# Copying two columns per VectorE instruction with and/xor and register-addressed scalars, in a graph-network kernel on one core

## The chip, the core and the metric

The kernel runs on one core of a Trainium2 chip. The metric is the device time of one execution in microseconds (us); lower is better. An engine is named as in the profile: PE (TensorE), PEld (its weight loads), DVE (VectorE), ACT (ScalarE), POOL (GpSimd) and SP (SyncE). A name with a q behind it (DVEq) is the sequencer of that engine, which carries out register loads, register operations and semaphore waits itself and hands the rest to the engine.

## What is computed

One layer of message passing over a graph with 12500 nodes of 64 features and 400000 edges with 16 attributes, followed by a residual sum and a layer norm. The edges are sorted by their target `dst`.

```python
m_in = concatenate([x[src], x[dst], edge_attr], axis=-1)
h = silu(m_in @ W1 + b1)
messages = silu(h @ W2 + b2)
agg = segment_sum(messages, dst, num_segments=12500)
y = silu(concatenate([x, agg], axis=-1) @ W3 + b3)
return layernorm(x + y)
```

What matters here is `x[src]`: the sources are random, so 400000 rows (or columns of the transposed x) have to be fetched by index.

## The kernel before

The edges are cut into 3125 tiles of 128, and eight tiles make an octet; the main loop runs over 391 octets (`NO`) and works ahead and behind: octet o is gathered three octets earlier, its first layer runs in iteration o, the second layer in o + 1, the sum over targets (`add_up`) in o + 2, and `add_window` adds that to the node sums `agg` in o + 4. The order of PE, ScalarE, VectorE and SyncE is written out by hand (`manual_schedule`): on each engine, instructions run in the order in which the loop calls them. What waits for what is kept by semaphores that the framework sets for every read after a write, also between two instructions of one engine.

The rows of x[src] come in three ways.

- `gather` (L373): POOL starts an indirect DMA for each tile, which fetches 128 rows from a table in DRAM. From octet 12 (`RAW`) that is `pa`, which already holds x times the first part of W1; the rows are added to the first layer's PSUM tile by products with the identity (L454).
- `columns`: for one pair of tiles (256 edges) in about every second octet there is no gather. All of x, transposed, is resident in SBUF twice (`xs`: partitions 0 to 63 and again 64 to 127, one column of 64 values per node). For each edge, ScalarE or VectorE copies that node's column into a tile `cx`, from an address in a register. PE multiplies `cx` by `w1d` (L451). `pairs` lists the octets that take a pair; `RATE` is the number of columns copied per octet, by both engines together, and so sets how often a pair is ready.
- `rows`: SyncE fetches single rows for a further 23 pairs by DMAs of 256 bytes (L324), 16 an octet.

`columns(o, eng, part)` is called twice per octet and engine: VectorE's part 0 comes after `compare_dst` (tile `oh`, L424), its part 1 after `window_copy` (`xw`, L402) and `compare_nodes` (`eh`, L430); ScalarE's part 0 comes ahead of the first layer's Silu (`h`, L458), part 1 ahead of the second layer's (`m`, L473). `ACOLS` and `VCOLS` give the columns of each part. A part is cut into pieces of at most 16 columns, for the first, and 8 for the others (`LOADS`), and where the tile of 128 edges ends. Per piece there is one register load (TENSOR_LOAD at L290) that reads the addresses from `cxi` into registers, and then one instruction per column: on VectorE a `tensor_reduce` (max over an axis of one element) of 4 bytes as uint8 (L297), on ScalarE a `copy` (L299).

`address` (L359) makes byte addresses of the indices on VectorE two octets earlier. `bases` (L381) loads the registers of four windows, every fourth octet. The nodes' own last layer and norm run in groups within the loop (L514 to L547): `node_stats` takes `bn_stats` (L533) and `bn_aggr` (L534) in turn, `divide` (L547) is a `tensor_scalar` with two scalars of one value per partition. `wrow` is a PSUM tile that holds small rows for the comparisons (`wn`, `row`); the gathers rotate through five buffers.

Of the kernel before, what the change touches and what calls it, by code (L numbers as in the profile page):

```python
# [11 lines left out]
I32 = mybir.dt.int32  # L12
U8 = mybir.dt.uint8
AF = mybir.ActivationFunctionType
OP = mybir.AluOpType
AX = mybir.AxisListType
PSUM = bass.MemoryType.PSUM
DRAM = bass.MemoryType.DRAM
ENG = mybir.EngineType

P = 128
# [3 lines left out]
S = 48  # L25
# [2 lines left out]
AHEAD = 3  # L28
RAW = 12
TABLES = 7  # L30
ACOLS = (32, 28)
VCOLS = (32, 32)
ROWS = 16
LOADS = (16, 8)
XBASE = (0, 64 << 18)
XADDR = 36864
LAG = CT * P // 32
# [7 lines left out]
def kernel(  # L45
# [43 lines left out]
    with ExitStack() as inner:  # L89
        windows(inner, tc, ident, badi, pa, x, xt, src_c, src_row, dst_c, dst_row, attr_t, dst_2, attr_2, base, w1, b1, w2, b2, w3, b3, out, edges)  # L90
# [7 lines left out]
def windows(ctx, tc, ident, badi, pa, x, xt, src_c, src_row, dst_c, dst_row, attr_t, dst_2, attr_2, base, w1, b1, w2, b2, w3, b3, out, edges):  # L98
    nc = tc.nc
    N, D = x.shape  # L100
# [3 lines left out]
    NO = base.shape[1]  # L104
# [31 lines left out]
    for s in range(2):  # L136
        h = slice(s * D, (s + 1) * D)
# [10 lines left out]
    for s in range(2):  # L148
        h = slice(s * D, (s + 1) * D)
# [6 lines left out]
    for s in range(3):  # L156
        part = const.tile([1, D], BF16, name=f"part{s}")
# [55 lines left out]
    wrow = wps.tile([P, 512], F32, name="wrow")  # L213
    wn, row = wrow[:, :NO], wrow[:, NO:NO + S]
    nc.vector.tensor_copy(row, rowi)
    pb = mis.tile([P, NO], F32, name="mm")
    nc.tensor.matmul(pb, ones, bf, start=True, stop=True)
    nc.vector.tensor_copy(wb, pb)
# [17 lines left out]
    for k in range(3):  # L236
        t = fast.tile([P, P], F32, name=f"xw{k}")
# [10 lines left out]
    with tc.tile_pool(name="gat", bufs=AHEAD + 2) as gat, tc.tile_pool(name="drp", bufs=2) as drp, \  # L248
# [11 lines left out]

        RATE = sum(ACOLS) + sum(VCOLS)
        pairs = []
        while True:
            o = RAW + -(-2 * P * (len(pairs) + 1) // RATE) + 1
# [3 lines left out]
        cols, indices = {}, {}  # L268
        xb = xs.bitcast(U8)

        def columns(o, eng, part):
            if o < RAW:
                return
            lo = (o - RAW) * RATE
            if eng == ENG.Activation:
                lo, n = lo + sum(ACOLS[:part]), ACOLS[part]
            else:
                lo, n = lo + sum(ACOLS) + sum(VCOLS[:part]), VCOLS[part]
            hi, todo = lo + n, n
            while lo < hi:  # L280
                j, e0 = lo // (2 * P), lo % (2 * P)
                if j >= len(pairs):
                    return
                n = min(hi - lo, P - e0 % P, LOADS[lo > hi - todo])
                if pairs[j] not in cols:
                    cols[pairs[j]] = cx.tile([P, P], F32, name="cx")
                t = cols[pairs[j]].bitcast(U8)
                s = e0 // P
                h = slice(s * D, (s + 1) * D)
                _, regs = nc.values_load_multi_w_load_instructions(  # L290
                    indices[j][0:1, e0:e0 + n], engines=(eng,), min_val=XBASE[s] + XADDR,
                    max_val=XBASE[s] + XADDR + 4 * (N - 1), skip_runtime_bounds_check_because="src names a node")
                for e, r in zip(range(e0 % P, e0 % P + n), regs):
                    to, frm = t[h, 4 * e:4 * e + 4], xb[h, ds(r - (XBASE[s] + XADDR), 4)]
                    if eng == ENG.DVE:

                        nc.vector.tensor_reduce(to, frm[:, :, None], AX.X, OP.max)  # L297
                    else:
                        nc.scalar.copy(to, frm)  # L299
                lo += n  # L300


        rpairs = []
        while True:
            o = RAW + -(-2 * P * (len(rpairs) + 1) // ROWS) + 1
# [128 lines left out]
        def first_layer(o):  # L434
            c, t0, n, first, last = octs[o]
            n2 = n + n % 2
            k = n2 // 2
            ga = got.pop(o)
            oh, eh = hots.pop(o)
            p1 = ps1.tile([P, OT // 2, P], F32, name="p1")  # L440
            nc.tensor.matmul(p1[:, :k], xw[o % 3], oh, start=True, stop=False, skip_group_check=True)  # L441
            if o < RAW:
                pt = mis.tile([P, OT // 2, P], F32, name="mm")
                for i in range(k):
                    nc.tensor.matmul(pt[:, i, :], ga[:, 2 * i:2 * i + 2, :].rearrange("p s d -> p (s d)"), ident,  # L445
                                     start=True, stop=True)
                xg = work.tile([P, OT // 2, P], F32, name="m")
                nc.vector.tensor_copy(xg[:, :k], pt[:, :k])
                nc.tensor.matmul(p1[:, :k], w1d, xg[:, :k], start=False, stop=True, skip_group_check=True)
            if o in pairs:  # L450
                nc.tensor.matmul(p1[:, 0, :], w1d, cols.pop(o), start=False, stop=False, skip_group_check=True)  # L451
            for i in range(1 if o in pairs else 0, k if o >= RAW else 0):
                g2 = single.pop(o) if o in rpairs and i == 1 else ga[:, 2 * i:2 * i + 2, :]
                nc.tensor.matmul(p1[:, i, :], g2.rearrange("p s d -> p (s d)"), ident,  # L454
                                 start=False, stop=(i == k - 1), skip_group_check=True)
            columns(o, ENG.Activation, 0)
            h = work.tile([P, OT // 2, P], F32, name="h")
            nc.scalar.activation(h[:, :k], p1[:, :k], AF.Silu, bias=b1s)  # L458
            made[o] = h, eh

        def second_layer(o):
            c, t0, n, first, last = octs[o]
            n2 = n + n % 2
            k = n2 // 2
            h, eh = made.pop(o)
            p2 = ps2.tile([P, OT, D], F32, name="p2")
            nc.tensor.matmul(p2[:, :n2, :], one3, b2r[:, :n2, :], start=True, stop=False, skip_group_check=True)  # L467
            for i in range(k):
                nc.tensor.matmul(p2[:, 2 * i:2 * i + 2, :].rearrange("p s d -> p (s d)"), h[:, i, :], w2d,  # L469
                                 start=False, stop=(i == k - 1), skip_group_check=True)  # L470
            columns(o + 1, ENG.Activation, 1)
            m = work.tile([P, OT, D], F32, name="m")
            nc.scalar.activation(m[:, :n2], p2[:, :n2], AF.Silu)  # L473
            made[o] = m, eh
# [85 lines left out]
        todo = {}  # L560
# [7 lines left out]
        for q in range(early):  # L568
            o = lead[due[q]] + 3 if q < rest else NO
# [4 lines left out]
        for q0, q1 in batches:  # L574
            o = lead[due[q1 - 1]] + 3
# [22 lines left out]
        with tc.manual_schedule(engines={ENG.PE, ENG.Activation, ENG.DVE, ENG.SP}):  # L598
            compare_dst(0)
            compare_nodes(0)  # L600
            for o in range(NO + 1):
# [3 lines left out]
                for k in parts[3 * o - 3:3 * o] if o else []:  # L605
                    n = min(XC, NP - k)
# [33 lines left out]
                if o + 1 < NO:  # L640
                    compare_dst(o + 1)
                columns(o, ENG.DVE, 0)
                if o < NO:
                    first_layer(o)
# [10 lines left out]
                if 30 <= o < 30 + 2 * LP and o % 2 == 0:  # L655
                    k = (o - 30) // 2
                    part = rel[:, k * TILES // LP:(k + 1) * TILES // LP]
# [307 lines left out]
```

## Time and profile before

| | |
|---|---|
| median of 3 runs | 3438.62 us (3430.88 to 3440.32) |
| the profiled execution's own time | 5200.1 us |
| its span, first to last instruction | 5197.9 us |
| busy in the span: PE, PEld | 2932.5 us, 2075.4 us |
| busy in the span: VectorE | 2641.3 us, 26395 instructions |
| busy in the span: ScalarE | 2906.1 us, 23402 instructions |
| busy in the span: POOL | 2565.3 us, 2724 instructions |
| gathers by POOL (from `pa` and from x) | 2619 and 96, mean 0.94 us each |
| column copies, VectorE and ScalarE | 24032 and 22560 |
| granted TensorE clock, mean | 0.629 |

The profiled execution took much longer than the others; a busy share of its span is not the share of a normal execution. In a row of the groups, the name says which tile is written and from what (`cx<-xs`), then come the count, the busy time, the mean duration of one, and the idle time of that engine just ahead of these instructions with what ended it. A duration runs from the start of an instruction[...], and the next one can start before that; what one costs in a row of equal ones is the time from start to start, the pitch. "issue" is idle time for which the profile shows no releaser.

### The profile page before, as it was taken

Reading aid. Unit: us, or ns where it says so; the run is one execution under the profiler, and the core shown is the slowest. Engines: PE = TensorE matmul, PEld = TensorE weight load, DVE = VectorE, ACT = ScalarE, POOL = GpSimd, SP = SyncE. Lnnn points to the kernel's source line nnn. Section 1 sums busy time; section 2 is a strip of 40 time slices with the busy share of each in tenths; the row PEclk is TensorE's granted clock in tenths of the full one; section 3 lists DMA queues with packets and bytes.
Section 4 is the critical chain, followed back from the end, with each engine's and each line's share of the span. In section 5 each row is a group of like instructions: output and inputs, shape, how many; then the busy total and the mean of one; then the engine's idle time right before and its main releaser. Section 6 shows DMA issues by size and latency. Waiting matters only on the chain. (4 is left out here: it accounts for less than half of the span.)

```text
span 5197.9 us, 107486 instructions
## 1 busy us (share of the span) xinstructions
PE 2932.5 (56%) x15131; PEld 2075.4 (40%) x15131; DVE 2641.3 (51%) x26395; ACT 2906.1 (56%) x23402; POOL 2565.3 (49%) x2724
## 2 busy tenths in 40 slices
PE   5655655555555555555564655656555555555566
PEld 3443434434433344343343434434433343344344
DVE  1255555545555555555555555555555555555555
ACT  1255555555555655655556565555556555655555
POOL 5544454454444544445444444545454444555453
PEclk7666565666666666666656566565656666665656
DMA  4321111211211121122112211211211221121121
GB/s 85 86 46 39 40 39 40 47 39 40 46 42 43 40 46 40 40 43 42 41 40 49 43 40 42 44 39 40 47 40 40 44 47 40 40 47 39 40 46 40
DMA packets 203943, 229.98 MB, mean 44 GB/s; under 512 B 133612, under 2 KB 141988, under 8 KB 202324
## 3 DMA queue, kind: packets, MB, share of 16 engines
q1 hardware_dynamic: 101528, 122.61, 10.5%
q0 software_dynamic: 86880, 89.14, 9.1%
q10 hardware_dynamic: 14812, 11.26, 0.9%
q14 instruction: 595, 4.87, 0.3%
q8 instruction: 128, 2.10, 0.2%
HBM read 216.36 MB, written 6.40 MB: 43 GB/s over the span
## 5 line engine op out<-in xcount | busy, mean ns | idle before, releaser
L373 POOL DMA_INDIRECT ga<-pa,sc x2619 | 2472.2, 944 | 2516.1 <-PE p L454 1699.8
L299 ACT COPY cx<-xs 64x4 uint8 x22560 | 2404.2, 188 | 1406.1 <-issue 1362.4
L297 DVE TENSOR_REDUCE cx<-xs 64x4 uint8 x24032 | 1910.3, 150 | 1806.6 <-issue 1740.9
L441 PE MATMUL p<-oh,xw 128*128 128x512 f32 (+1 forms) x782 | 772.4, 1089 | 1529.3 <-DVE xw L402 727.6
L441 PEld LDWEIGHTS p<-oh,xw 128*128 128x128 f32 x782 | 187.1, 297 | 1637.1 <-DVE xw L402 776.3
L482 PE MATMUL pg<-eh,m 128*64 128x48 f32 x6250 | 363.0, 277 | 588.6 <-ACT m L473 174.1
L454 PEld LDWEIGHTS p<-ident,ga 128*128 128x128 f32 x2620 | 591.3, 314 | 194.9 <-issue 193.6
L469 PE MATMUL p<-w2d,h 128*128 128x128 f32 x3126 | 642.0, 369 | 1.5 <-issue 1.4
L469 PEld LDWEIGHTS p<-w2d,h 128*128 128x128 f32 x3126 | 545.3, 263 | 133.0 <-issue 133.0
L454 PE MATMUL p<-ident,ga 128*128 128x128 f32 x2620 | 593.2, 397 | 0.0
L482 PEld LDWEIGHTS pg<-eh,m 128*64 128x64 f32 x6250 | 312.1, 189 | 680.2 <-issue 342.2
L473 ACT ACTIVATE m<-p 128x512 f32<-128x512 f32 x391 | 231.8, 593 | 474.9 <-remote 308.9
L458 ACT ACTIVATE h<-p,b1s 128x512 f32<-128x512 f32 x391 | 267.4, 684 | 319.0 <-remote 138.6
L402 DVE TENSOR_TENSOR xw<-mm,mask 96x128 f32<-96x128 f32 x391 | 110.4, 282 | 439.9 <-issue 392.4
L397 PE MATMUL mm<-w1bb,xr 64*96 64x128 f32 x782 | 241.0, 401 | 72.6 <-ACT z L523 49.9
L424 DVE TENSOR_TENSOR oh<-dr,wrow 96x512 f32<-96x512 int32 x391 | 263.6, 674 | 6.3 <-issue 3.5
L430 DVE TENSOR_TENSOR eh<-wrow,dc 128x384 f32<-128x384 f32 x391 | 213.2, 545 | 42.2 <-issue 42.2
L467 PE MATMUL p<-b2r,one 3*128 3x512 bf16 x391 | 194.5, 498 | 0.0
L451 PEld LDWEIGHTS p<-cx,w1d 128*128 128x128 f32 x364 | 116.0, 319 | 175.4 <-issue 175.4
L397 PEld LDWEIGHTS mm<-w1bb,xr 64*96 64x96 f32 x782 | 127.8, 214 | 144.7 <-issue 68.7
L487 DVE TENSOR_TENSOR agg<-agg,pg 128x48 f32 x391 | 77.3, 198 | 123.4 <-remote 32.3
L373 POOL DMA_INDIRECT ga<-in_x,sc x96 | 91.0, 948 | 63.5 <-PE mm L445 28.9
(81 smaller groups left out, 802.7 us busy)
## 6 DMA issues: line engine op xcount, KB each, us to landing
rx<-pa SPq DMA_DIRECT2D x5888, 0.2 KB
dr<-in_dst SPq DMA_DIRECT2D x260, 288.0 KB
ga<-pa,sc POOLq DMA_INDIRECT x2619
oh<-in_attr SPq DMA_DIRECT2D x130, 192.0 KB
xr<-in_xt SPq DMA_DIRECT2D x391, 24.0 KB
xs<-in_xt ACTq DMA_DIRECT2D x12, 512.0 KB
pa<-v ACTq DMA_DIRECT2D x12, 256.0 KB
xa<-in_x SPq DMA_DIRECT2D x24, 128.0 KB
```

Of the source, the lines that this page charges most:

```text
L297: nc.vector.tensor_reduce(to, frm[:, :, None], AX.X, OP.max)
L299: nc.scalar.copy(to, frm)
L373: nc.gpsimd.indirect_dma_start(out=ga[:, i, :], out_offset=None, in_=x if o < RAW else pa[:, :], in_offset=bass.IndirectOffsetOnAxis(ap=sc ...
L397: nc.tensor.matmul(pw[:E, :], winrow[o].rearrange("k s w -> k (s w)"), w1bb.rearrange("k s m -> k (s m)"), start=True, stop=True)
L424: nc.vector.tensor_tensor(oh[:E, :], dr[:, e:e + w], wn[:E, o:o + 1].to_broadcast([E, w]), op=OP.is_equal)
L430: nc.vector.tensor_tensor(eh[:, :n], row[:, None, :].to_broadcast([P, n, S]), rel[:, t0:t0 + n, None].to_broadcast([P, n, S]), op=OP.is_equal)
L441: nc.tensor.matmul(p1[:, :k], xw[o % 3], oh, start=True, stop=False, skip_group_check=True)
L454: nc.tensor.matmul(p1[:, i, :], g2.rearrange("p s d -> p (s d)"), ident, start=False, stop=(i == k - 1), skip_group_check=True)
L458: nc.scalar.activation(h[:, :k], p1[:, :k], AF.Silu, bias=b1s)
L469: nc.tensor.matmul(p2[:, 2 * i:2 * i + 2, :].rearrange("p s d -> p (s d)"), h[:, i, :], w2d, start=False, stop=(i == k - 1), skip_group_ch ...
L473: nc.scalar.activation(m[:, :n2], p2[:, :n2], AF.Silu)
L482: nc.tensor.matmul(pg[s * D:(s + 1) * D, :], m[:, i, :], eh[:, i, :], start=(i < 2), stop=(i >= n - 2), skip_group_check=True)
```

## The change

On VectorE one instruction now makes two columns. `first` is a pair of integers in `wrow`, all ones and zero. A `tensor_scalar` reads these two elements and applies `and` with the first column and `xor` with the second; both columns are scalars of one value per partition whose address comes from a register. It writes (a xor b, b) into two neighbouring columns of `cx`. At the end of each piece one `tensor_tensor` applies `xor` to all even and odd columns of the piece, in place, which turns a xor b into a. VectorE copies 76 columns an octet instead of 64, ScalarE 68 instead of 60, all pieces have up to 16 columns, and the register load of a piece is issued right after the instructions of the piece before it, across the parts too, and no longer just ahead of its own.

```diff
-ACOLS = (32, 28)
-VCOLS = (32, 32)
+ACOLS = (36, 32)
+VCOLS = (40, 36)
-LOADS = (16, 8)
+LOADS = 16
...
+    first = wrow[:, NO + S:NO + S + 2].bitcast(I32)
+    nc.vector.memset(wrow[:, NO + S:NO + S + 2], 0.0)
+    nc.vector.tensor_scalar(first[:, 0:1], first[:, 0:1], -1, None, op0=OP.bitwise_or)
...
+        def addresses(eng, j, e0, n):
+            s = e0 // P
+            _, regs = nc.values_load_multi_w_load_instructions(
+                indices[j][0:1, e0:e0 + n], engines=(eng,), min_val=XBASE[s] + XADDR,
+                max_val=XBASE[s] + XADDR + 4 * (N - 1), skip_runtime_bounds_check_because="src names a node")
+            return regs
+
+        def columns(o, eng, part):
+
+            batch = list(pieces(o, eng, part))
+            coming = batch + list(pieces(o + part, eng, 1 - part))[:1]
+            for i, (j, e0, n) in enumerate(batch):
+                regs = ahead.pop((eng, j, e0), None) or addresses(eng, j, e0, n)
...
-                for e, r in zip(range(e0 % P, e0 % P + n), regs):
-                    to, frm = t[h, 4 * e:4 * e + 4], xb[h, ds(r - (XBASE[s] + XADDR), 4)]
-                    if eng == ENG.DVE:
-
-                        nc.vector.tensor_reduce(to, frm[:, :, None], AX.X, OP.max)
-                    else:
-                        nc.scalar.copy(to, frm)
+                es = range(e0 % P, e0 % P + n)
+                if eng == ENG.Activation:
+                    for e, r in zip(es, regs):
+                        nc.scalar.copy(t[h, 4 * e:4 * e + 4], xb[h, ds(r - (XBASE[s] + XADDR), 4)])
+                else:
+
+                    def column(r):
...
+                        return xb[h, ds(r - (XBASE[s] + XADDR), 4)].bitcast(I32)
+                    ti = cols[pairs[j]].bitcast(I32)
+                    for e, ra, rb in zip(es[::2], regs[::2], regs[1::2]):
+                        nc.vector.tensor_scalar(ti[h, e:e + 2], first[h, :], column(ra), column(rb),
+                                                op0=OP.bitwise_and, op1=OP.bitwise_xor)
+                    both = ti[h, es[0]:es[0] + n].rearrange("p (c s) -> p c s", s=2)
+                    nc.vector.tensor_tensor(both[:, :, 0], both[:, :, 0], both[:, :, 1], op=OP.bitwise_xor)
+                if i + 1 < len(coming):
+                    ahead[(eng, *coming[i + 1][:2])] = addresses(eng, *coming[i + 1])
```

More of the change, by code (lines that the diff above doesn't have):

```diff
@@ L269, in windows, with pieces @@
         xb = xs.bitcast(U8)
-        def columns(o, eng, part):
+        def pieces(o, eng, part):
             if o < RAW:
@@ L278, in columns @@
                 lo, n = lo + sum(ACOLS) + sum(VCOLS[:part]), VCOLS[part]
-            hi, todo = lo + n, n
+            hi = lo + n
             while lo < hi:
@@ L283, in columns @@
                     return
-                n = min(hi - lo, P - e0 % P, LOADS[lo > hi - todo])
+                n = min(hi - lo, P - e0 % P, LOADS)
+                yield j, e0, n
+                lo += n
+        ahead = {}
+        def addresses(eng, j, e0, n):
[9 more added lines that the diff above has]
+                regs = ahead.pop((eng, j, e0), None) or addresses(eng, j, e0, n)
                 if pairs[j] not in cols:
@@ L289, in columns @@
                 h = slice(s * D, (s + 1) * D)
-                _, regs = nc.values_load_multi_w_load_instructions(
-                    indices[j][0:1, e0:e0 + n], engines=(eng,), min_val=XBASE[s] + XADDR,
-                    max_val=XBASE[s] + XADDR + 4 * (N - 1), skip_runtime_bounds_check_because="src names a node")
-                for e, r in zip(range(e0 % P, e0 % P + n), regs):
-                    to, frm = t[h, 4 * e:4 * e + 4], xb[h, ds(r - (XBASE[s] + XADDR), 4)]
-                    if eng == ENG.DVE:
-                        nc.vector.tensor_reduce(to, frm[:, :, None], AX.X, OP.max)
-                    else:
-                        nc.scalar.copy(to, frm)
-                lo += n
+                es = range(e0 % P, e0 % P + n)
[4 more added lines that the diff above has]
+                    def column(r):
+                        r = r.with_bounds(min_val=XBASE[s] + XADDR, max_val=XBASE[s] + XADDR + 4 * (N - 1),
+                                          guaranteed_mod_val=XADDR % 4, out_of_modulus=4)
+                        return xb[h, ds(r - (XBASE[s] + XADDR), 4)].bitcast(I32)
[7 more added lines that the diff above has]
+                    ahead[(eng, *coming[i + 1][:2])] = addresses(eng, *coming[i + 1])
         rpairs = []
```

## The prediction

> **What bounds the kernel now.** I read the page's costliest groups first, then the waits, then single stretches of the timeline and the rows of single lines, VectorE's sequencer (DVEq) among them.
>
> ```profile
> span 5197.9 us, 107486 instructions
> ...
> L373 POOL DMA_INDIRECT ga<-pa,sc x2619 | 2472.2, 944 | 2516.1 <-PE p L454 1699.8
> L299 ACT COPY cx<-xs 64x4 uint8 x22560 | 2404.2, 188 | 1406.1 <-issue 1362.4
> L297 DVE TENSOR_REDUCE cx<-xs 64x4 uint8 x24032 | 1910.3, 150 | 1806.6 <-issue 1740.9
> ```
> The profiled execution took 5200.1 us (span 5197.9), 51% more than the median of 3438.6, so its span can't be the base of a sum. The extra time is the idle time put down to "issue": 1362 us on ScalarE and 1741 us on VectorE, in which a column copy waits for nothing shown. I take those stalls as the recording's own (the median could not hold them), and take durations only from stretches without them.
>
> ```profile
> 2999.35 0.94 POOL L373 DMA_INDIRECT ga<-pa,sc  x1 [0.30 <-issue]
> ...
> 3000.60 0.94 POOL L373 DMA_INDIRECT ga<-pa,sc  x1 [0.30 <-issue]
> ...
> 3001.84 0.94 POOL L373 DMA_INDIRECT ga<-pa,sc  x1 [0.30 <-issue]
> ```
> Gathers that wait for nothing start 1.247 us apart. There are 2619 + 96 = 2715: 2715 x 1.247 = 3385.6 us. The first starts at 2.8 us; that leaves 50 us of the median for what follows the last one (54.5 us in the profile). So the unprofiled kernel is bound by POOL nearly from end to end, 3385.6 / 391 = 8.66 us an octet.
>
> How far behind are the others? These rows give VectorE's costs:
>
> ```profile
> 3008.98 0.59 DVE L297 TENSOR_REDUCE cx<-xs 64x4 uint8 x8 [0.15 <-issue]
> ...
> 3010.43 0.34 DVE L359 TENSOR_SCALAR cxi<-cxi 1x128 int32<-1x128 int32 x2
> ```
> ```profile
> 1477.23 0.98 DVE L547 TENSOR_SCALAR v<-v,mv,rstd 128x64 f32<-128x64 f32 x4
> ```
> ```profile
> L290 DVEq TENSOR_LOAD <-cxi x2391: 340/597/1340, 221.4 to 5159.0; - x200
> ```
> Eight reductions in 0.59 us, the last 0.14 long: 0.064 us from start to start. The loads of column addresses into registers (TENSOR_LOAD, on VectorE's sequencer) take 0.345, 0.595 and 1.098 us for 4, 8 and 16 registers: 0.094 + 0.0628 n. After a load of 8 the next load starts 0.33 us later, so the sequencer hands on a column in about 0.041 us. VectorE's columns now: 2391 loads, 24032 columns: 2391 x 0.094 + 24032 x 0.0628 + 24032 x 0.041 = 2719 us, over the 376 octets that have them 7.2 us an octet; its other work runs beneath the loads. The shortest octets of the trace (start of one L458 activation to the next) are 7.0 to 7.2 us, which agrees. ScalarE: 24 copies in 2.38 us, 0.094 us apart, x 60 + 0.68 + 0.60 for h and m = 6.9 us. Slack beneath POOL: about 1.4 us an octet.
>
> **The change part by part.**
>
> *Gathers.* A rate of 144 columns an octet instead of 124 makes 211 column pairs of tiles instead of 182 (same loop, same limit of 376 octets), so 58 gathers fewer: 58 x 1.247 = 72 us less for POOL, 2657 gathers, 8.47 us an octet. No DMA but these goes or moves; PE exchanges 58 transposing products for 29 L451 products, nothing.
>
> *ScalarE.* 68 columns x 0.094 + 1.28 = 7.7 us, still below 8.47. Its loads (0.305, 0.547, 1.015 us for 4, 8, 16) run beneath the copies; those that now come ahead of h and m no longer stand behind PE's semaphore. I cost this at nothing; the cover is POOL's 8.47 us (margin 0.8 us) or, below, VectorE's much longer octet.
>
> *The pair instruction.* 28500 columns become 14250 tensor_scalars with two pointer scalars. The nearest row is L547: TENSOR_SCALAR with two pointers, four in 0.98 us, the last 0.307 long: 0.223 us from start to start. It streams 64 elements. An element takes 1.04 ns (L430 with 384 has a pitch of 0.463, L424 with 512 one of 0.596), but L359, a tensor_scalar in SBUF as L547 is, does 128 in a pitch of 0.132, of which 0.064 is the reduction's floor: half that, 0.52 ns. So L547's 64 take 33 ns, and a two-element instruction with two pointers costs 0.223 - 0.033 = 0.190 us. Bounds: 0.223 (nothing taken off) and 0.156 (67 ns off, at 1.04 each); the one-pointer L230 (5 elements, 0.227 us against 0.153 for L202 without one) puts a pointer at 0.07 and favours 0.190. That is 0.095 us a column against 0.064: on the engine the pair is dearer, not cheaper. 14250 x 0.190 = 2708 us.
>
> The Trainium skill (Perfetto Trace Analysis, Optimizing Scalar/DVE Operations) puts VectorE's fixed cost at some 60 ns for SBUF and 125 ns for PSUM; `first` lies in PSUM. By that the pitch is 0.255 and the total below rises by 14250 x 0.065 = 926 us. But here L430 reads `row` from PSUM and the next instruction follows after 0.463 us for 384 elements (0.400 at 1.04 ns), 0.063 over. I follow the trace: no PSUM price.
>
> *The xor, and what queues behind it.* Each piece ends in a tensor_tensor that reads what the last pair just wrote, on the same engine. L533 and L534 are such a chain: L534 waits for L533's semaphore and starts 0.034 us after its end. Behind the xor in program order stands the register load of the next piece. What a sequencer instruction does behind a waiting engine instruction, the same place shows (bn_aggr L534, then the load of the windows' bases L381):
>
> ```profile
> 1251.82 0.18 DVE L534 BATCH_NORM_AGGREGATE mv<-st 128x2 f32<-128x6 f32 x1
> 1251.92 0.19 DVE L533 BATCH_NORM_STATS2 st<-v 128x6 f32<-128x64 f32 x1
> 1252.15 0.18 DVE L534 BATCH_NORM_AGGREGATE mv<-st 128x2 f32<-128x6 f32 x1
> ```
> ```profile
> L381 DVEq TENSOR_LOAD <-bi x1: 347/347/347, 1252.2 to 1252.2; - x1
> ```
> The load starts at 1252.162, 0.015 us after the last waiting L534 is let go, though the sequencer had nothing else to do. In 23 of the 26 such places the next load or register operation starts 0.013 to 0.015 us after the last L534; in the other three nothing followed for 0.8 us or more. At 68.7 us the same load starts 0.020 us after an L448 that waited 32.5 us for PE. The skill's lifecycle of a DVE instruction (Perfetto Trace Analysis, Per-instruction lifecycle) says the reverse as I read it: once an instruction is pushed into the wait queue, the sequencer is ready for the next. By that rule the loads run beneath the pairs (rival B, 3955 us); by the trace they are held. The trace decides.
>
> So a piece is serial: load, 0.088 us to the first column, the pairs, 0.074 us by which a result comes later than the pitch (L547: 0.297 - 0.223), 0.034 for the semaphore, 0.015 to the next load: 0.211 us of seams. Counting the pieces as the loops cut them (the same count for before gives the trace's 2391 loads exactly): 2250 on VectorE, 1406 of 16, 188 of 12, 281 of 8, 375 of 4.
>
> - loads: 2250 x 0.094 + 28500 x 0.0628 = 2001 us
> - pairs: 14250 x 0.190 = 2708 us
> - seams: 2250 x 0.211 = 475 us
> - the rest. The moved load now stands ahead of xw and eh, and ahead of agg and oh, which the sequencer can hand on only after it; before, the load ran beneath them (at 3010.56 one starts just ahead of oh at 3010.81). By pitch: xw 0.20, eh 0.46, oh 0.60, agg 0.115, its register operation and semaphore 0.12, address scaling 0.15, bases 0.09, node groups 0.17: 1.9 us x 376 = 716 us
>
> Sum 5900 us for 376 octets, 15.7 us an octet against 8.47 for POOL: VectorE becomes the bound, by far, and who waits for it is PE at L441 (for xw and oh), then ScalarE, then POOL for gather buffers. Ahead lie 2.8 + 12 x 8 x 1.247 = 122 us without columns, behind about 50 us: 5900 + 122 + 50 = 6072. I say 6070 us. With the pitch at 0.156 it is 5590, at 0.223 6540.
>
> *Small ones.* The two instructions that make `first` (0.06 + 0.16 us) lie in the start, ahead of POOL's own pace: nothing. The xor reads two SBUF inputs; L530 does too, and beside its nine places among gathers the median spacing stays 1.248 us, the worst is 1.79. Even 0.14 us for each of six xors an octet would leave POOL at 9.3 us, covered by 15.7. Without that cover it would cost 2250 x 0.14 = 315 us at worst.
>
> **The rivals.** (About 0.3% is what a measurement of this kernel can tell from no change.)
>
> A, faster: VectorE's octet fits beneath POOL's. The sequencer goes on past the waiting xor, so that the reordered loads vanish beneath the pairs, and the engine alone counts: 37.9 pairs + 6 xors of 0.182 (latency, semaphore, own pitch) + 1.77. This stays below 8.47 if a pair costs under 0.148 us. Then the gathers' saving is whole: 3438.6 - 72 = 3366 us. Against it: 23 held loads, and 0.223 in L547. With the loads held it is out whatever a pair costs: loads, seams and the rest alone are (2001 + 475 + 716) / 376 = 8.5 us. For it: register-addressed scalars are in no row of the trace.
>
> B, loads not held, pair at 0.190: 37.9 x 0.190 + 1.09 + 1.77 = 10.06 us an octet, 3783 + 172 = 3955 us. This is also what comes out if the change doesn't do what it says and no semaphore is set before the xor.
>
> C, held, but pointers nearly free (pitch 0.066, the reduction's): 5900 - 14250 x 0.124 + 172 = 4305 us. Only L547 and L230 speak against it.
>
> **How the numbers follow.** My forecast 0.76, B 0.08, C 0.06, A 0.09, no change 0.01. Faster 0.09, same 0.01, slower 0.90. The range from 4300 to 6600 takes in the forecast with both ends of the pitch (5590, 6540) and C; it leaves out A, B and no change, 0.18.
>
> **What would show it.** Right: TENSOR_SCALAR cx x14250 with 0.19 us from start to start and a mean of 0.26 to 0.28; TENSOR_TENSOR cx x2250; 2250 DVEq loads, each starting some 0.015 us after an xor starts, with VectorE idle beneath it; gathers 2561 + 96 with most of POOL's idle time released by PE; PE at L441 waiting for xw. Wrong: loads that overlap pairs (A or B), a pitch near 0.07 (C), or POOL with no idle time (A).

## The result, and the profile after

The changed kernel takes 6289.25 us (median, 6276.68 to 6290.12), the kernel before 3439.32 in the same comparison: the ratio is 1.829, with a 95% interval from 1.825 to 1.833. The forecast was 6070, between 4300 and 6600. The profiled execution took 6276.7 us (span 6274.9), so this time the profile and the times agree.

The page of the changed kernel, the rows that answer to those of before (POOL's gathers, the columns on ScalarE, the columns on VectorE), and the row of the closing xors:

```profile
span 6274.9 us, 102223 instructions
...
L401 POOL DMA_INDIRECT ga<-pa,sc x2561 | 2423.9, 946 | 3657.3 <-PE p L482 2979.2
L323 DVE TENSOR_SCALAR cx<-wrow,xs 64x2 int32<-64x2 int32 x14250 | 2978.3, 288 | 1160.6 <-issue 1122.3
L314 ACT COPY cx<-xs 64x4 uint8 x25516 | 2546.3, 188 | 19.2 <-issue 1.6
...
L326 DVE TENSOR_TENSOR cx<-cx 64x8 int32<-64x8 int32 x2250 | 362.2, 161 | 77.3
```

POOL now stands idle for 3657 us in front of its gathers, and PE's release of a gather buffer ends most of that. The waits lead on from there to VectorE. In each line the waiting engine comes first, then the one it waited for, the total, how often and the longest:

```profile
POOL ga L401 <- PE p L482: 2979.2, 368, 14.5
...
PEld p L469 <- DVE xw L430: 1477.3, 352, 6.3
...
PE pg L510 <- DVE agg L515: 1370.5, 321, 6.7
```

VectorE hardly waits for another engine (no such entry is above 71 us): its largest is "issue", 1122 us in front of pairs. A stretch of its timeline shows what that is (start, duration, what, count, and in brackets the idle time ahead):

```profile
3002.51 0.16 DVE L326 TENSOR_TENSOR cx<-cx 64x8 int32<-64x8 int32 x1
3003.22 0.83 DVE L323 TENSOR_SCALAR cx<-wrow,xs 64x2 int32<-64x2 int32 x4 [0.55 <-issue]
3004.09 0.15 DVE L326 TENSOR_TENSOR cx<-cx 64x4 int32<-64x4 int32 x1
3005.29 0.29 DVE L430 TENSOR_TENSOR xw<-mm,mask 96x128 f32<-96x128 f32 x1 [1.04 <-issue]
3005.50 0.54 DVE L458 TENSOR_TENSOR eh<-wrow,dc 128x384 f32<-128x384 f32 x1
3005.96 1.57 DVE L323 TENSOR_SCALAR cx<-wrow,xs 64x2 int32<-64x2 int32 x8
3007.57 0.16 DVE L326 TENSOR_TENSOR cx<-cx 64x8 int32<-64x8 int32 x1
```

The register load that belongs into the first gap is in the row of its line for that moment:

```profile
L295 DVEq TENSOR_LOAD <-cxi x1: 599/599/599, 3002.5 to 3002.5; - x1
```

The xor of a piece of 16 starts at 3002.511, the load of the next 8 addresses at 3002.526. The load ends at 3003.125, and the first pair starts at 3003.220. In between the engine has the 0.16 us of the xor and nothing else. So it goes all through: 2038 of the 2250 loads start within 0.03 us after an xor starts, and not one pair starts while a load runs. Of these 2038 loads 1827 have no semaphore to wait for in the trace's records, while every xor has one: what holds them is the xor in front. The other loads but one (211) stand behind a semaphore instruction of their own, for a new tile of addresses, and start some 0.08 us after the xor.

In e1 to e4 VectorE, ScalarE and SyncE stalled again and again, with some 0.7 us from one start to the next, as in the profiled execution of before, and the kernel before beside them took mostly 5252 to 5278 us; beside e5 to e12 it took 3429 to 3437 us, and only times of these are compared.

### The profile page after: what moved, and what is told of

The parts are those of the page before. It is cut to its first block, busy times and chain, and to the rows that moved or that the text cites. A ratio compares the mean times of both kernels' runs of the same rounds, so it can differ in the third digit from the quotient of the medians.

```text
span 6274.9 us, 102223 instructions
## 1 busy us (share of the span) xinstructions
PE 3274.1 (52%) x15131; PEld 2314.6 (37%) x15131; DVE 4086.2 (65%) x18923; ACT 3064.0 (49%) x26358; POOL 2517.0 (40%) x2666
## 5 line engine op out<-in xcount | busy, mean ns | idle before, releaser
L401 POOL DMA_INDIRECT ga<-pa,sc x2561 | 2423.9, 946 | 3657.3 <-PE p L482 2979.2
L323 DVE TENSOR_SCALAR cx<-wrow,xs 64x2 int32<-64x2 int32 x14250 | 2978.3, 288 | 1160.6 <-issue 1122.3
L314 ACT COPY cx<-xs 64x4 uint8 x25516 | 2546.3, 188 | 19.2 <-issue 1.6
L510 PE MATMUL pg<-eh,m 128*64 128x48 f32 x6250 | 415.9, 303 | 1587.4 <-DVE agg L515 1370.5
L510 PEld LDWEIGHTS pg<-eh,m 128*64 128x64 f32 x6250 | 364.2, 215 | 1683.6 <-issue 851.1
L497 PE MATMUL p<-w2d,h 128*128 128x128 f32 x3126 | 792.3, 433 | 0.0
L497 PEld LDWEIGHTS p<-w2d,h 128*128 128x128 f32 x3126 | 679.1, 320 | 165.6 <-issue 165.6
L326 DVE TENSOR_TENSOR cx<-cx 64x8 int32<-64x8 int32 x2250 | 362.2, 161 | 77.3
L425 PE MATMUL mm<-w1bb,xr 64*96 64x128 f32 x782 | 282.6, 462 | 32.0 <-DMA xr<-in_xt 21.1
L387 DVE TENSOR_SCALAR cxi<-cxi 1x128 int32<-1x128 int32 x422 | 86.8, 250 | 228.2 <-DVEq L295 200.7
```

The source lines that it names most:

```text
L314: nc.scalar.copy(t[h, 4 * e:4 * e + 4], xb[h, ds(r - (XBASE[s] + XADDR), 4)])
L323: nc.vector.tensor_scalar(ti[h, e:e + 2], first[h, :], column(ra), column(rb), op0=OP.bitwise_and, op1=OP.bitwise_xor)
L326: nc.vector.tensor_tensor(both[:, :, 0], both[:, :, 0], both[:, :, 1], op=OP.bitwise_xor)
L401: nc.gpsimd.indirect_dma_start(out=ga[:, i, :], out_offset=None, in_=x if o < RAW else pa[:, :], in_offset=bass.IndirectOffsetOnAxis(ap=sc ...
L425: nc.tensor.matmul(pw[:E, :], winrow[o].rearrange("k s w -> k (s w)"), w1bb.rearrange("k s m -> k (s m)"), start=True, stop=True)
L510: nc.tensor.matmul(pg[s * D:(s + 1) * D, :], m[:, i, :], eh[:, i, :], start=(i < 2), stop=(i >= n - 2), skip_group_check=True)
```

## The experiments

**e6: more pieces.** The changed kernel with twice as many waits.

```diff
-LOADS = 16
+LOADS = 8
```

> The changed kernel with pieces of at most 8 columns in place of 16: 3844 pieces on VectorE instead of 2250, so 1594 more register loads, waits and xors; columns, pairs and rates are the same. Theory T (load, pairs and seam in series): each further piece costs the fixed part of a load and the seam, 0.094 + 0.211 us, so 6289 + 486 = 6775 us. Rival R1 (pairs' time on the engine is the cause, waits cost only the xor's own pitch of 0.07 to 0.16 us): 6400 to 6540 us. Rival R6 (shorter pieces share out better among other waits): no more than 6290.

6792.65 us. Against 6289.25 that is 503 us for 1594 more pieces, 0.316 us each, where 0.305 was expected; R1 would have given half at most. The wait and the load are in series, and a piece costs about what the prediction's seam and the fixed part of a load make. (The changed kernel's own seam, measured below, is longer, 0.247 us; but behind four pairs, as here, the last result in the upper half of the partitions comes 0.114 us later than the pitch, behind eight 0.156.)

**e1 and e9: the load ahead of the xor.** The same two statements in the other order; nothing else differs.

```diff
-                    both = ti[h, es[0]:es[0] + n].rearrange("p (c s) -> p c s", s=2)
-                    nc.vector.tensor_tensor(both[:, :, 0], both[:, :, 0], both[:, :, 1], op=OP.bitwise_xor)
                 if i + 1 < len(coming):
                     ahead[(eng, *coming[i + 1][:2])] = addresses(eng, *coming[i + 1])
+                if eng == ENG.DVE:
+                    both = ti[h, es[0]:es[0] + n].rearrange("p (c s) -> p c s", s=2)
+                    nc.vector.tensor_tensor(both[:, :, 0], both[:, :, 0], both[:, :, 1], op=OP.bitwise_xor)
```

> The changed kernel, with the register load of the next piece issued ahead of the piece's xor instead of behind it; the arithmetic is the same. Theory T (the load is held behind the waiting xor, and load, pairs and seam are in series): a load of 16 (1.1 us) now runs beneath eight pairs (1.5 us) and only the loads behind pieces of 4 and 8 columns stick out (about 1.1 us an octet), so VectorE's octet falls from 16.3 to 10 to 11.3 us and the time to 4000-4400 us. Rival R1 (the pairs' own time on the engine is the cause and the loads are hidden anyway): the time stays near 6290 us. Rival R2 (the pointer reads get in the way of loads, so that the two can't run side by side): no less than 5800 us.

> The same kernel as in the first experiment (the register load of the next piece ahead of the xor), run again where, it is hoped, the stalls of 0.7 us[...] are absent. Theory T: the loads run beneath the pairs and 4000-4400 us remain, about 2000 us less than the changed kernel. Rival R1 (pairs alone): 5800 us or more. If the stalls are there again (the kernel before at 5260 us), near 5380 us as in the first run, and nothing is told.

With stalls (e1) it took 5377.48 us, which tells nothing of the total. Its trace already tells the mechanism: successive loads of 16 addresses start as little as 1.5 us apart, in the changed kernel never less than 2.81. Without stalls (e9) it took 4483.78 us: 1805 us gone by the order of two statements. The rows of the pairs and of the xors in e9:

```profile
span 4479.7 us, 102223 instructions
...
L323 DVE TENSOR_SCALAR cx<-wrow,xs 64x2 int32<-64x2 int32 x14250 | 2966.3, 287 | 11.9 <-issue 0.7
...
L329 DVE TENSOR_TENSOR cx<-cx 64x8 int32<-64x8 int32 x2250 | 366.7, 163 | 332.1 <-DVE cx L323 274.0
```

As many pairs with the same duration as in the changed kernel, but the idle time ahead of them is 11.9 us instead of 1160.6. On average 3.5 pairs start while a load runs, and 1 load of 2250 sees none. R1 and R2 are out. The total lies 84 us above T's range: VectorE is idle for 332 us in front of the xors. The row puts most of that down to the last pair, but in the trace 256 us of it lie where a load of 16 follows the pairs of a piece of 4 or 8 columns; the pairs are done first, and the xor, behind the load in the order, starts 0.09 us after the load ends. And each xor still holds the engine until its last pair is done.

**e2 and e10: no closing xor.** The pair has `and` in both places; the kernel leaves out the xor, and with it the true columns.

```diff
-                                                op0=OP.bitwise_and, op1=OP.bitwise_xor)
-                    both = ti[h, es[0]:es[0] + n].rearrange("p (c s) -> p c s", s=2)
-                    nc.vector.tensor_tensor(both[:, :, 0], both[:, :, 0], both[:, :, 1], op=OP.bitwise_xor)
+                                                op0=OP.bitwise_and, op1=OP.bitwise_and)
```

> The changed kernel without the closing xor of each piece; the pair takes and in both places (so even columns hold a and b, odd ones zero: this part of the computation is changed). Nothing on VectorE now waits for a pair within a piece. Theory T: no load is held, the engine alone counts: 37.9 x 0.19 + 1.77 = 9.0 us an octet, 9.0-9.7 with loads that stick out, so 3550-3850 us. Rival R1 (pairs alone): only the xors' own pitch goes, 2250 x 0.16 = 360 us, near 5930 us.

> The same kernel as in the second experiment (no xor at the end of a piece; and in both places of the pair, which changes that part of the computation), run again without stalls. Theory T: VectorE's engine alone, 37.9 x 0.193 + 1.9 = 9.2 us an octet, 3550-3850 us. Rival R1 (pairs alone): 5930 us. With stalls 5370 us again.

5367.61 us with stalls, 3763.91 us without: inside the range of T. The row of the pairs in e10:

```profile
span 3757.4 us, 100321 instructions
...
L323 DVE TENSOR_SCALAR cx<-wrow,xs 64x2 int32<-64x2 int32 x14250 | 2861.8, 310 | 11.7 <-issue 0.5
```

So the xor with its wait costs 2525 us of the 6289. Of this the held load is 1805 (e9); the other 720 are what the xor still costs in e9: its own time, its wait for the last pair, and the loads that stick out.

**e3 and e11: reductions instead of pairs.** Rates, pieces and order of loads as changed.

```diff
-                    for e, ra, rb in zip(es[::2], regs[::2], regs[1::2]):
-                        nc.vector.tensor_scalar(ti[h, e:e + 2], first[h, :], column(ra), column(rb),
-                                                op0=OP.bitwise_and, op1=OP.bitwise_xor)
...
+                    for e, r in zip(es, regs):
+                        nc.vector.tensor_reduce(t[h, 4 * e:4 * e + 4], xb[h, ds(r - (XBASE[s] + XADDR), 4)][:, :, None], AX.X, OP.max)
```

> The changed kernel with the pairs and xors put back to one tensor_reduce a column; the rates of 68 and 76 columns, the pieces of 16 and the loads issued behind each piece stay. Theory T: no wait, so loads overlap with columns already handed on; VectorE's sequencer needs 76 x 0.104 + 6 x 0.094 + 0.25 = 8.7 us an octet against POOL's 8.47, so 3370-3500 us, close to the kernel before. Rival R3 (the higher rate or the order of the loads makes the loss): above 4500 us.

> The same kernel as in the third experiment (76 and 68 columns, order of the loads and pieces as changed, but one tensor_reduce a column and no xor), run again without stalls. Theory T: VectorE's sequencer needs 76 x 0.104 + 6 x 0.094 + 0.4 = 8.9 us an octet, 3460-3600 us: the pair with its xor makes nearly the whole loss. Rival R3 (rates or order of the loads): above 4500 us. With stalls 5820 us again.

5826.44 us with stalls; 3981.27 us without, 381 us above the range. Two things follow. The rates, the pieces and the order of the loads are by themselves a loss of 549 us against the kernel before (one from the other they were not told apart). And e10, with pairs, is 217 us faster than this: by time alone a pair without its closing xor is no bad bargain, since loads hide beneath it (in e10 4.1 pairs start while a load runs, on average, and VectorE is idle for only 11.7 us in front of its pairs).

The expectation had left out the work that the prediction calls "the rest". The trace of e11 has it: from the start of a load of 16 to the next load it takes 1.67 us where only columns lie between, but 2.33 us where xw and eh follow the load and 2.77 us where agg and oh do (medians). In the old order, in e5, it is 1.66 us at both places. The moved loads of 16 cost 0.66 + 1.10 = 1.8 us an octet: xw, eh, agg and oh now stand behind the load in the sequencer's order.

**e4: one pointer.** The second column is left out of the pair.

```diff
-                        nc.vector.tensor_scalar(ti[h, e:e + 2], first[h, :], column(ra), column(rb),
-                                                op0=OP.bitwise_and, op1=OP.bitwise_xor)
+                        nc.vector.tensor_scalar(ti[h, e:e + 2], first[h, :], column(ra), None, op0=OP.bitwise_and)
```

> The changed kernel with pairs that have only the and with the first column; the second column is left out (that part of the computation is missing), its address is still loaded and the closing xor stays. Theory T (each pointer scalar costs 0.062 us on the engine): pitch 0.128 us instead of 0.19, so 14250 x 0.062 = 880 us less, near 5400 us. Rival R4 (the pitch is set by the read from PSUM or by handing on the instruction, not by pointers): pitch 0.19 and 6290 us as before. Rival R5 (the first pointer sets up most of it): pitch 0.15-0.18.

5761.76 us, with stalls, so the total is not read. The pitch is, from VectorE's timeline:

```profile
2999.89 1.21 DVE L323 TENSOR_SCALAR cx<-wrow,xs 64x2 int32<-64x2 int32 x8
...
3006.95 1.09 DVE L323 TENSOR_SCALAR cx<-wrow,xs 64x2 int32<-64x2 int32 x8
```

Eight in 1.09 us, of which the last is about 0.20, are 0.127 us from start to start (0.126 to 0.134 in most of the trace, up to 0.145 in the first step of a piece) against 0.188 to 0.194 with two pointers: 0.06 us a pointer, as T had it from L547. R4 and R5 are out. The second operation went with the second column, but an operation alone costs nothing that can be seen: in the kernel before, L359 (two operations with constants, 128 elements) has a pitch of 0.131 us and L340 (one, 256 elements) 0.198, which 0.064 us and 0.52 ns an element give for both. A register-addressed scalar costs what the prediction took from fixed ones, and `first` in PSUM adds nothing that can be seen: 0.127 is the reduction's 0.064 and one pointer.

**e5: the kernel before without SyncE's rows**, made to learn what the stalls are.

```diff
         rpairs = []
-        while True:
...
-            rpairs.append(o)
```

> The kernel before without SyncE's single rows: their 23 pairs of tiles are gathered by POOL like the others (46 gathers more), the arithmetic is the same. It asks what the idle time under 'issue' is, since the kernel before took 5250 to 5280 us in the runs of the first experiments, as in its profiled execution, and not 3439. Theory S (in such runs instructions of all engines together are held to some 20.7 per us, 107486 in 5198 us, by the recording): some 12000 of SyncE's instructions go, so 95000 / 20.7 = 4600 us. Rival S2 (the stalls belong to VectorE and ScalarE, or to addresses from registers): no gain, 5260 us or 57 us more for the gathers. If this call's runs are without stalls, 3439 + 57 = 3496 us.

There were no stalls here, so S and S2 stay undecided. But 3490.72 us against 3433.90 are the 57 us for 46 gathers that were worked out, as they should be if POOL's count of gathers sets the time of the kernel before. The profiled execution shows it outright:

```profile
span 3488.6 us, 95162 instructions
...
L368 POOL DMA_INDIRECT ga<-pa,sc x2665 | 2518.3, 945 | 812.0 <-issue 714.5
L299 ACT COPY cx<-xs 64x4 uint8 x22560 | 2217.5, 188 | 143.6 <-issue 119.7
```

POOL's idle time is its own issue between gathers; with it, 2760 spacings (median 1.249 us) fill 3449 of 3489 us.

**e7, e8 and e12: looking for a version that gains.** e7 is e9's order with one xor for a whole part (and each tile), and 64 columns on VectorE, 68 on ScalarE; e8 has the same columns by reductions, as in e3; e12 has 68 on VectorE (`VCOLS = (36, 32)`) and 64 on ScalarE (`ACOLS = (32, 32)`) by reductions. Of the edits only the columns of e7 and e8 are shown:

```diff
-VCOLS = (40, 36)
+VCOLS = (32, 32)
```

> The changed kernel mended: the loads come ahead of the xor, one xor closes a whole part (and each tile) instead of each piece, and VectorE takes 32 columns a part (16 + 16) so that its octet fits; ScalarE keeps 68: 132 columns an octet, 193 pairs. Theory T: VectorE's octet is 32 x 0.19 + 2.2 x 0.18 + 1.9 = 8.4 us beneath POOL's 8.59; without stalls 3439 - 22 x 1.247 = 3412 us (3400-3480). Where instructions of all engines together are held to some 20 per us: about 98000 instructions, 4700-5000 us, faster than the kernel before at 5264. In the trace, starts of successive loads of 16 some 1.5 us apart. Rival R1 (pairs too dear at any order): above 5300 us with stalls.

> The same 132 columns (68 on ScalarE, 64 on VectorE in pieces of 16) and the loads issued behind each piece, but one tensor_reduce a column as in the kernel before: the change's rates and order of loads without its pair. Theory T: no waits, VectorE's sequencer needs 64 x 0.104 + 4.4 x 0.094 + 0.25 = 7.3 us an octet, so POOL sets the time: 3412 us without stalls. Where instructions of all engines together are held to some 20 per us: about 110000 instructions, 5300-5600 us, slower than the mended pair kernel. Rival R3 (the order of the loads harms): 3450 us or more, or 5700 us or more with stalls.

> 132 columns an octet by tensor_reduce as in the eighth experiment, but 64 on ScalarE and 68 on VectorE instead of 68 and 64, since ScalarE (68 x 0.0945 + 1.28 + 0.3 = 8.0 us, before the nodes' extra) seemed to be what held POOL there. Theory T2: ScalarE 7.6, VectorE 8.0, POOL 8.59 us an octet: POOL is the bound and 22 gathers fewer give 3434 - 27 = 3407 us (3395-3425). Rival R7 (POOL is held by VectorE's order of the loads, which stand ahead of xw and oh, not by ScalarE): 3460 us or more. With stalls 5300-5600 us.

| | us | ratio to before (95%) |
|---|---|---|
| e7, pairs, 64 + 68 | 3524.19 | 1.026 (1.024 to 1.027) |
| e8, reductions, 64 + 68 | 3462.10 | 1.009 (1.007 to 1.011) |
| e12, reductions, 68 + 64 | 3654.27 | 1.065 (1.063 to 1.067) |

None gains, and all three miss what was worked out for them. e7 lies 44 us above its range: VectorE is busy for 3277.6 of 3522 us, and from its first pair to its last an octet takes 8.9 us where 8.4 were worked out, so there is no room left beneath POOL's 8.59. e8 lies 50 us above T, on the side of R3 (the order of the loads). In e12, T2 fails and R7 holds: four columns moved from ScalarE to VectorE cost 192 us, 0.51 us an octet, which is four columns at 0.104 and a further load at 0.094. That fits a bound by VectorE's sequencer, though the engine is busy for only 2533.6 of 3654 us. Whether a higher rate with the old order of loads would gain was not tried.

## Why the prediction was right

Its mechanism is the one that the runs show, point by point.

- The load held behind the waiting xor: seen 2038 times, priced by e6, undone by e9. What the prediction took from 23 bn_aggr instructions holds for 2250 xors, and the rule that it set aside, a sequencer free once an instruction is in the wait queue, would have given 3955 us.
- Loads: 2001 us predicted, 2004 us in the trace.
- Pairs: pitch 0.190 predicted, 0.255 by the estimate with a price for PSUM that it set aside; 0.188 in the lower half of the partitions, 0.194 in the upper (medians), so 2722 us against 2708. Only the mean duration, 0.288 us, lies above the 0.26 to 0.28 that were named as a sign, since results in the upper half come later.
- Seams: 0.211 us predicted; measured 0.092 to the first pair (0.087 or 0.096, where nothing lies between), 0.034 for the semaphore, 0.014 to the load, and a last result that comes 0.074 us (lower half) or 0.140 us (upper half, mean) later than the pitch: 0.247 us on average, 556 us against 475.
- The rest: 1.9 us an octet predicted. From the first load (141.7 us) to the last pair (6232.8) are 6091 us; less loads, pairs and seams, 809 us stay, 2.2 us an octet. Nearly all of it can be seen: 762 pieces, two an octet, begin more than 0.11 us after their load, 778 us in all.
- Start 142 us against 122, end 44 against 50.

The differences (3 + 14 + 81 + 93 + 20 - 6) add up to the 205 us between 6072 and the profiled 6276.7, as they must where one term is what the others leave. The start, 20 us late, was not traced further.

Two statements did not hold. The stalls of the profiled execution of before were put down to the recording; but e5's profiled execution has none, and the kernel before beside e1 to e4 had them in every run. Nor are they on all engines: POOL's gathers keep their 1.25 us in them. What makes them stays open. The method, to sum only stretches without them, was not touched by that. And rival B was too low as a price of "not held": e9, where loads are not held but the xor stays, took 4484 us and not 3955, 332 us of that in front of xors, most of it because short pieces don't cover a load of 16. Without the xor it is 3764.

The gathers fell by 58 as forecast, but POOL, idle for 3657 us in front of them, was no longer the bound, so nothing came of it.

## What to carry to other kernels

On VectorE here, the sequencer's own work (register loads, register operations) stood still behind an engine instruction that waited for a semaphore, also where it waited only for its own engine's last result (2038 loads, each let go with the xor). So put the loads for the next batch ahead of the instruction that waits, and ahead of as little other work as possible. Two results per instruction are worth it only if operands are cheaper than instructions: here each scalar of one value per partition cost as much (0.063 us) as a whole small reduction (0.064).

## What was not expected of the hardware

- The same pair takes 0.188 us from start to start in partitions 0 to 63 and 0.194 in 64 to 127; in a run of eight in the upper half, the durations grow by some 0.010 us from each to the next (0.290 to 0.353 us from 3009.72 on), in the lower half not (0.26 us). What makes it was not tried.
